# Attention block: the last three queries leave the passage as raw products and are normalised during attention's steps 3 to 10

## The chip, the cores and the metric

One Trainium2 chip, one of its NeuronCores, one launch. A core has five engines, each with its own instruction queue worked off in order: TensorE (PE: matrix products and transposes, written to PSUM), VectorE (DVE) and ScalarE (ACT) for element-wise work, GpSimd (POOL), and SyncE (SP), which here only issues DMA transfers. Engines wait for each other with semaphores. The metric is device time in microseconds (us) of the whole launch, lower is better.

## What is computed

Four layers, each added to its input x of 64 batches x 64 tokens x 512 features, all in float32. The change concerns the third, windowed attention over a paged key/value cache. Cut to what matters:

```python
x = x + x @ W[id] + b[id]                         # layer 0: a matrix per batch
x = x + x @ W1.T + low-rank update of an adapter  # layer 1
# layer 2: 8 query heads in 4 groups, head size 64
q = (x @ Wq.T), k = (x @ Wk.T), v = (x @ Wv.T)
q = q * rsqrt(mean(q * q, -1) + 1e-6) * (1 + q_norm_scale)   # per head
q = concat([q1 * cos - q2 * sin, q2 * cos + q1 * sin])       # halves rotated by position
k = the same with k_norm_scale
put k and v at their places in the cache
scores = q @ k_all.T * 256 ** -0.5, masked to a window of 256 positions
x = x + (softmax(scores) @ v_all) @ Wo.T
x = x + per-batch 64x64 matrix over the token axis + bias    # layer 3
```

## The kernel before

The 4096 tokens are 32 tiles of 128 tokens (two batches each), `NT = 32`. The program has three parts.

*The first part* (`layer0`, `layer1`, `keep_kv` and others, about 518 us) loads a matrix per batch, computes layers 0 and 1, keys and values of each tile, and the queries of tiles 0 to 24. Keys and values go to `kvd` in DRAM, turned queries to `qTd` in DRAM.

*The passage* is the loop `for i in range(NT - LATE + 1, NT - 1)` (LATE is 8): the queries of tiles 25 to 30. For each: `product` makes four matmuls of 128x512 into a PSUM bank (line 140); `turned` (lines 116 to 135) normalises and rotates: ScalarE squares it (L120), VectorE sums each head's squares (L122), ScalarE takes the root (L123), VectorE inverts it (L126) and multiplies (L128); then two half-width products with the sine (L133), one with the cosine (L134), and a sum into `qr` (L135). `turned` is a generator that stops twice, so that the caller can place its parts between other work. `turn_q` transposes `qr` with four TensorE operations (L174), copies the result with ScalarE (L177) and stores it in `qTd` (L181, SP's queue).

*Attention* has 32 steps, one per tile. Step `s` on TensorE, in this order: `scores(s)` (8 matmuls, L842), `attend(s - 1)` (48 short ones, L889), in even steps from 4 on `last(s - 4)` (layer 3), `project(s - 2)` (L917), `keys(s + 1)` (transposes of the next tile's keys, L823, L829), and `turn(s)` (transposes of the softmax weights, L875, L879). Beside it VectorE subtracts the maximum (L850), normalises the weights (`normalise`, L862, L866), adds the residual into `x3` (L921) and copies half of the transposed weights (`pT`, L876); ScalarE takes exponentials (L854) and copies keys (`kT`) and the other weights. GpSimd issues the gathers of keys and values for tile `s + 2` (`load_kv`, five indirect DMAs, L769) and adds a unit matrix to layer 3's matrix `w3` (L815). SP issues the loads of masks (`load_mask`), queries (`load_q`), residual and `w3` (`load_pair`).

Tile 31's query is made in step 0 into the one bank of the pool `pyp`, which `project` uses as well (tile `py`), its norm is spread over steps 1 to 3 and its turn is in step 5. Tile 29's turn is in step 0, tile 30's in step 4. All other PSUM tiles take turns in a ring of seven banks (`bank`). The order on all engines is the order of the program text (`manual_schedule`).

Of the kernel before, what the change touches and what calls it, by code (L numbers as in the profile page):

```python
# [12 lines left out]
F32 = mybir.dt.float32  # L13
I32 = mybir.dt.int32
AF = mybir.ActivationFunctionType
ALU = mybir.AluOpType
AX = mybir.AxisListType
# [3 lines left out]
B, T, D = 64, 64, 512  # L21
# [4 lines left out]
H, G, HD = 8, 4, 64  # L26
BLOCK, NBLK, WINDOW = 16, 257, 256
HALF = HD // 2
# [21 lines left out]
LATE = 8  # L50
NT = NTOK // 128
# [3 lines left out]
def bc(ap, shape):  # L55
    return ap.to_broadcast(list(shape))
# [3 lines left out]
def body(ctx: ExitStack, tc: tile.TileContext, a: dict, out: bass.AP):  # L60
    nc = tc.nc
    V, S, P, TE = nc.vector, nc.scalar, nc.gpsimd, nc.tensor
# [27 lines left out]
    late = ctx.enter_context(tc.tile_pool(name="late", bufs=1))  # L90
    wq = late.tile([128, KC, D], F32, name="wq")
    gain = late.tile([128, 2, 2, HALF], F32, name="gain")
    gsw = late.tile([128, 2, 2, HALF], F32, name="gsw")
    epst = late.tile([128, 1], F32, name="epst")

    ring = ctx.enter_context(tc.tile_pool(name="ring", bufs=7, space=PSUM))
    pyp = ctx.enter_context(tc.tile_pool(name="pyp", bufs=1, space=PSUM))
# [5 lines left out]
    x2s, qrs, trig = {}, {}, {}  # L103

    def gains(kind, i, pool, X):

        cg = pool.tile([128, HD], F32, name=f"cg{kind}", bufs=2 if kind else LATE)
        sg = pool.tile([128, HD], F32, name=f"sg{kind}", bufs=2 if kind else LATE)
        for t, gn, tr in ((cg, gain, "cos"), (sg, gsw, "sin")):
            X.tensor_tensor(  # L110
                t.rearrange("p (h f) -> p h f", h=2), gn[:, kind],
                bc(trig[tr, i // 8][:, i % 8 : i % 8 + 1, :], [128, 2, HALF]), ALU.mult,
            )
        return cg, sg

    def turned(ps, n, to, pool, X, kind, cg, sg):

        psv = ps[:, : n * HD].rearrange("p (h d) -> p h d", d=HD)
        sq = pool.tile([128, n, HD], F32, name=f"sq{kind}", bufs=2)
        S.activation(sq, psv, AF.Square)  # L120
        ss = pool.tile([128, n], F32, name=f"ss{kind}", bufs=2)
        V.tensor_reduce(ss, sq, AX.X, ALU.add)  # L122
        S.activation(ss, ss, AF.Sqrt, bias=epst, scale=1.0 / HD)  # L123
        yield
        rs = pool.tile([128, n], F32, name=f"rs{kind}")
        V.reciprocal(rs, ss)  # L126
        qn = pool.tile([128, n, HD], F32, name=f"qn{kind}", bufs=2)
        V.tensor_tensor(qn, psv, bc(rs[:, :, None], [128, n, HD]), ALU.mult)  # L128
        yield
        t2 = sq  # L130
        for f in range(2):
            fs, of = slice(f * HALF, (f + 1) * HALF), slice((1 - f) * HALF, (2 - f) * HALF)
            V.tensor_tensor(t2[:, :, fs], qn[:, :, of], bc(sg[:, None, fs], [128, n, HALF]), ALU.mult)  # L133
        V.tensor_tensor(qn, qn, bc(cg[:, None, :], [128, n, HD]), ALU.mult)  # L134
        X.tensor_tensor(to, qn, t2, ALU.add)  # L135

    def product(i, w, name, pool=None):
        ps = pool.tile([128, 512], F32, name="py") if pool else bank(name)
        for c in range(KC):
            TE.matmul(ps, x2s[i][:, c, :], w[:, c, :], start=c == 0, stop=c == KC - 1)  # L140
        return ps

    def parts_q(i, pq, X, cs=None):
        qr = late.tile([128, H, HD], F32, name="qr", bufs=2)
        qrs[i] = qr.rearrange("p h d -> p (h d)")
        return turned(pq, H, qr, late, X, 0, *(cs or gains(0, i, late, X)))

    def copies(to, pool, ahead):

# [16 lines left out]
    def run(parts):  # L166
        for _ in parts:
            pass

    def turn_q(i, pool=late):  # L170
        qrf = qrs.pop(i)
        pqt = bank("pqt")
        for c in range(KC):
            TE.transpose(pqt[:, c * 128 : (c + 1) * 128], qrf[:, c * 128 : (c + 1) * 128], ident)  # L174
        qT = pool.tile([128, 2, 2, 2, T], F32, name="qTs", bufs=2 if pool is late else 4)
        for gp in range(2):
            S.copy(  # L177
                qT[:, gp].rearrange("p b h t -> p h b t"),
                pqt[:, gp * 256 : (gp + 1) * 256].rearrange("p (h b t) -> p h b t", h=2, b=2),
            )  # L180
        nc.sync.dma_start(  # L181
            qTd[i * 128 : (i + 1) * 128, :], qT.rearrange("p g b h t -> p (g b h t)")
        )

    with ExitStack() as pa:
# [494 lines left out]
        for c in range(KC):  # L680
            cs = slice(c * 128, (c + 1) * 128)
# [27 lines left out]
        for g in range(NG - 1):  # L709
# [5 lines left out]
            n, m = len(tiles[g]), len(tiles[g + 1])  # L715
            for k in range(m):
                i0, i = tiles[g + 1][k], tiles[g][k * n // m] if (k + 1) % (m // n) == 0 else None
# [9 lines left out]
                if q is not None:  # L727
                    pq = product(q, wq, "pq")
# [11 lines left out]
        i = NT - LATE  # L740
        run(parts_q(i, product(i, wq, "pq"), P))
        made.append(i)
        cs = {i: gains(0, i, late, P) for i in range(NT - LATE + 1, NT)}
        while len(made) > 1:
            turn_q(made.pop(0))
# [15 lines left out]
    bp = ctx.enter_context(tc.tile_pool(name="bp", bufs=2))  # L761

    kvs, kTs, mbs, prs, pTs, oTs, qTs, pairs, x3s = {}, {}, {}, {}, {}, {}, {}, {}, {}

    def load_kv(i):
        kv = kvs[i] = kvp.tile([128, 5, 2 * G * HD], F32, name="kv")
        for n in range(5):
            at = idxn[:, n % 2, 2 * i + n // 2 :][:, :1] if n < 4 else idxh[:, i : i + 1]
            P.indirect_dma_start(  # L769
                out=kv[:, n, :], out_offset=None, in_=kvd,  # L770
                in_offset=bass.IndirectOffsetOnAxis(ap=at, axis=0),
            )
# [6 lines left out]
    def load_q(i, queue=nc.sync):  # L779
        qT = qTs[i] = bp.tile([128, 2, 2, 2, T], F32, name="qT", bufs=4)  # L780
        queue.dma_start(
            qT.rearrange("p g b h t -> p (g b h t)"), qTd[i * 128 : (i + 1) * 128, :]
        )

    def load_mask(i):
        mb = mbs[i] = bp.tile([128, 2, NPOS], F32, name="mb", bufs=3)
        for h in range(2):
            r = nc.sync.value_load(cut[0:1, 2 * i + h : 2 * i + h + 1], min_val=0, max_val=WINDOW - 1)
            if h == 0:
                nc.sync.dma_start(mb[:, 0, :], maskd[:, bass.ds(r, NPOS)])  # L790
            else:
                nc.sync.dma_start(mb[:, 1, T:], maskd[:, bass.ds(r, WINDOW)])
                nc.sync.dma_start(mb[:, 1, :T], maskd[:, WINDOW:][:, bass.ds(r, T)])
# [23 lines left out]
    def keys(i):  # L817
        kv = kvs[i]
        kT = kTs[i] = bp.tile([128, 2, 2 * NPOS], F32, name="kT")
        for gp in range(2):  # L820
            pk = bank("pkt")
            for n, c in enumerate((0, 1, 4)):
                TE.transpose(pk[:, n * 128 : (n + 1) * 128], kv[:, c, gp * 128 : (gp + 1) * 128], ident)  # L823
            S.copy(kT[:, gp, :384], pk[:, :384])
        pk = bank("pkt")
        for gp in range(2):
            for c in range(2):
                n = 2 * gp + c
                TE.transpose(pk[:, n * 128 : (n + 1) * 128], kv[:, 2 + c, gp * 128 : (gp + 1) * 128], ident)  # L829
        S.copy(kT[:, :, 384:], pk.rearrange("p (g n) -> p g n", g=2))  # L830
# [128 lines left out]
    load_q(0)  # L959
    load_mask(0)  # L960

    parts = {}
    for i in range(NT - LATE + 1, NT - 1):
        pq = product(i, wq, "pq")
        parts[i] = parts_q(i, pq, V, cs[i])
        next(parts[i])
        if i > NT - LATE + 2:
            turn_q(i - 2, bp)
        if i - 1 in parts:
            run(parts.pop(i - 1))  # L970
        next(parts[i])
    keys(0)
    load_q(1)
    load_mask(1)
    wo = bp.tile([128, KC, D], F32, name="wo", bufs=1)
    for s in range(NT):
        if s + 2 < NT:
            if s < 2:
                after_keys(s)
            load_kv(s + 2)  # L980
            load_mask(s + 2)
        if s and s + 2 < NT:
            load_q(s + 2)
        scores(s)
        if s >= 2:
            add_one(s - 2)
        if s:
            load_pair(s - 1)
            attend(s - 1)
        else:  # L990

            parts[NT - 1] = parts_q(NT - 1, product(NT - 1, wq, "pq", pyp), V, cs[NT - 1])
            turn_q(NT - 3, bp)
        if s == 2:
            next(parts[NT - 1])
        normalise(s, 0)
        normalise(s, 1)
        if s % 2 == 0 and s >= 4:
            last(s - 4)
        if s >= 2:  # L1000
            project(s - 2)
        if s + 1 < NT:
            keys(s + 1)
        if s in (4, 5):
            turn_q(NT - 6 + s, bp)
        elif s in (2, 3):

            run(parts.pop(NT - 4 + s))
        turn(s)
        if s == 0:  # L1010
            load_q(2)
            nc.sync.dma_start(wo, a["woT"].rearrange("(c p) f -> p c f", p=128))
        elif s == 1:
            next(parts[NT - 1])
    i = NT - 1
    load_pair(i)
    add_one(i - 1)
# [60 lines left out]
```

## Time and profile before

| | us |
|---|---|
| median of 3 runs | 974.5 (lowest 973.77, highest 974.64) |
| the profiled execution, with what lies around it | 969.85 |
| its span, first to last instruction | 967.9 |
| its mean granted TensorE clock | 0.995 |
| first scores of step 0, 1, 2, 3, 4 (start) | 543.78, 554.31, 565.86, 585.69, 597.45 |
| later steps, odd / even | about 11.8 / 13.6 each |

A line of the profile's timeline holds start, length, engine, line of the program, operation, `out<-in` by the program's names, shapes, how many merged instructions, and in brackets the engine's idle time before it with what ended that idle time. A matmul in float32 is recorded as two instructions. TensorE's weight loads (PEld) lie beside its matmuls.

### The profile page before, as it was taken

The numbers are of one execution on the slowest core, as the hardware profiler recorded it, in microseconds if no ns is written. First come the engines' busy times: TensorE is split into PE (matmuls) and PEld (weight loads), VectorE is DVE, ScalarE is ACT, GpSimd is POOL, SyncE is SP. The second block draws the span as 40 slices with busy tenths as digits, with TensorE's granted clock in tenths as the row PEclk, the third lists the DMA queues.
The fourth block names the chain that finished last, engine by engine and source line by source line (L and its number), as shares of the span: only waits on it lengthen the run. The fifth ranks groups of instructions, "written<-read, shape, count | busy, mean of one in ns | idle before, by whom it ended". The sixth has DMA issues, their size and how long they took to land.

```text
span 967.9 us, 17784 instructions
## 1 busy us (share of the span) xinstructions
PE 930.5 (96%) x5397; PEld 506.6 (52%) x5397; DVE 608.7 (63%) x1736; ACT 412.9 (43%) x1084; POOL 404.8 (42%) x599
## 2 busy tenths in 40 slices
PE   5999999999999999999999979999999999999998
PEld 2443443444444444444444556766666666666665
DVE  3756898878573362552226858666667776667673
ACT  0212133232341322422223666656666666666663
POOL 3344265555453454444425543344444333334400
PEclk9999999999999999999999989999999999999999
DMA  7998999999999999999953774766665566566621
GB/s 251 342 324 304 376 375 324 377 393 320 396 330 383 392 339 389 387 351 389 372 218 125 235 261 135 217 214 205 204 194 185 181 194 197 191 204 202 197 69 45
DMA packets 133344, 260.97 MB, mean 270 GB/s; under 512 B 32737, under 2 KB 41570, under 8 KB 133250
## 3 DMA queue, kind: packets, MB, share of 16 engines
q1 hardware_dynamic: 108562, 178.61, 51.6%
q0 software_dynamic: 23280, 79.84, 24.8%
q10 hardware_dynamic: 1408, 1.39, 0.5%
q8 instruction: 43, 0.70, 0.3%
q14 instruction: 51, 0.42, 0.1%
HBM read 190.29 MB, written 69.50 MB: 268 GB/s over the span
## 4 chain that ended last, share of the span: by engine, by line
PE 73%; DVE 2%; ACT 1%; issue 1%; POOL 0%; ACTq 0%
PE py L917 12%; PE po L889 8%; PE ps L842 8%; PE p L635 7%; PE pk L140 7%; PE pq L140 7%; PE p L249 6%; PE ppt L875 6%; PE pkt L823 2%; PE ppt L879 2%; PE pkt L829 1%; PE pz L929 1%; PE pqt L174 1%; DVE pT L876 1%; PE pt L273 1%; PE px L654 1%
## 5 line engine op out<-in xcount | busy, mean ns | idle before, releaser
L769 POOL DMA_INDIRECT kv<-kvd,idxn x128 | 126.6, 989 | 211.1 <-PE po L889 166.9
L854 ACT ACTIVATE pr<-pr,mx 128x320 f32<-128x320 f32 x256 | 140.1, 550 | 7.0 <-DVE mx L850 2.9
L249 PE MATMUL p<-w,xt 128*64 128x512 f32 x512 | 122.2, 606 | 8.5 <-DMA w<-in_W 8.3
L917 PE MATMUL py<-wo,oT 128*128 128x512 f32 (+1 forms) x264 | 118.3, 592 | 1.7 <-DVE qn L128 1.7
L140 PE MATMUL pk<-wkv,x 128*128 128x512 f32 x256 | 115.4, 595 | 2.1 <-ACT x L656 2.1
L155 POOL DMA_INDIRECT st<-in_kvc,cidx x68 | 69.8, 1027 | 107.4 <-DMA kvd<-st 94.3
L635 PE MATMUL p<-w,x 128*128 128x512 f32 x256 | 113.6, 601 | 0.0
L140 PE MATMUL pq<-wq,x 128*128 128x512 f32 x248 | 111.3, 593 | 0.0
L850 DVE CUSTOM_DVE_ANT_0 pr<-ps,mb 128x320 f32<-128x320 f32 x256 | 107.8, 486 | 5.5 <-PE ps L842 2.9
L842 PE MATMUL ps<-kT,qT 64*128 64x320 f32 x512 | 86.9, 459 | 10.9 <-DVE pT L876 6.3
L876 DVE COPY pT<-ppt 128x512 f32<-128x512 f32 x64 | 41.9, 687 | 73.7 <-PE ppt L879 34.5
L866 DVE TENSOR_SCALAR pr<-pr,sm 128x320 f32<-128x320 f32 x256 | 85.4, 395 | 2.2
L889 PE MATMUL po<-pT,kv 128*64 128x128 f32 (+1 forms) x1536 | 84.1, 280 | 1.5 <-issue 1.5
L274 DVE TENSOR_TENSOR x<-pt,x 128x512 f32<-128x512 f32 x32 | 22.0, 688 | 100.6 <-PE pt L273 88.4
L889 PEld LDWEIGHTS po<-pT,kv 128*64 128x64 f32 (+1 forms) x1536 | 70.5, 137 | 22.1 <-DVE mx L850 13.6
L917 PEld LDWEIGHTS py<-wo,oT 128*128 128x128 f32 x264 | 47.5, 189 | 61.5 <-issue 58.4
L635 PEld LDWEIGHTS p<-w,x 128*128 128x128 f32 x256 | 48.3, 192 | 59.0 <-issue 56.7
L249 PEld LDWEIGHTS p<-w,xt 128*64 128x64 f32 x512 | 35.9, 138 | 78.3 <-issue 72.3
L135 POOL TENSOR_TENSOR qr<-qn,sq 128x512 f32<-128x512 f32 x25 | 31.7, 1267 | 105.5 <-DVE qn L134 105.5
L140 PEld LDWEIGHTS pk<-wkv,x 128*128 128x128 f32 x256 | 46.3, 190 | 50.4 <-issue 47.3
L140 PEld LDWEIGHTS pq<-wq,x 128*128 128x128 f32 x248 | 44.9, 190 | 46.2 <-issue 46.2
L842 PEld LDWEIGHTS ps<-kT,qT 64*128 64x128 f32 x512 | 45.2, 187 | 41.4 <-DVE pT L876 20.8
(191 smaller groups left out, 1317.9 us busy)
## 6 DMA issues: line engine op xcount, KB each, us to landing
w<-in_W SPq DMA_DIRECT2D x62, 1024.0 KB
kvd<-st SPq DMA_DIRECT2D x68, 512.0 KB
xt<-in_xT SPq DMA_DIRECT2D x32, 256.0 KB
x2d<-x2n SPq DMA_DIRECT2D x32, 256.0 KB
kvd<-kvn SPq DMA_DIRECT2D x32, 256.0 KB
qTd<-qTs SPq DMA_DIRECT2D x32, 256.0 KB
qT<-qTd SPq DMA_DIRECT2D x32, 256.0 KB
x2r<-x2d SPq DMA_DIRECT2D x32, 256.0 KB
```

The costliest lines, as they stand in the source:

```text
L140: TE.matmul(ps, x2s[i][:, c, :], w[:, c, :], start=c == 0, stop=c == KC - 1)
L155: P.indirect_dma_start(out=st, out_offset=None, in_=a["kvc"].rearrange("(n r) d -> n (r d)", r=2), in_offset=bass.IndirectOffsetOnAxis(ap= ...
L249: TE.matmul(p0[hs, :], xs[i][:, c, hs], w0s[i][h][:, c, :], start=c == 0, stop=c == KC - 1)
L635: TE.matmul(p1[i], x1s[i][:, c, :], w1[:, c, :], start=c == 0, stop=False)
L769: P.indirect_dma_start(out=kv[:, n, :], out_offset=None, in_=kvd, in_offset=bass.IndirectOffsetOnAxis(ap=at, axis=0),)
L842: TE.matmul(ps[g2][:, :NPOS], qT[rows, gp, b2].rearrange("p h t -> p (h t)"), kT[rows, gp, b2 * NPOS : (b2 + 1) * NPOS], start=True, stop= ...
L850: V.tensor_tensor_reduce(out=p, in0=ps[g2][:, :NPOS], in1=mb[:, b2, :], scale=-1.0, scalar=3.0e38, op0=ALU.add, op1=ALU.min, accum_out=mx[ ...
L854: S.activation(p, p, AF.Exp, bias=mx[:, g, b2 : b2 + 1], scale=-1.0, accum_out=sm[:, g, b2 : b2 + 1],)
L866: V.tensor_scalar(p, p, sm[:, g, b2 : b2 + 1], None, ALU.mult)
L875: TE.transpose(pt[:, n * 128 : (n + 1) * 128], pr[:, g, at : at + 128], ident)
L889: TE.matmul(po[b2][g2 * 64 : (g2 + 1) * 64, gp * 128 : (gp + 1) * 128], kv[rows, n, (G + g) * HD : (G + g + 1) * HD], pT[rows, c, m * 128 ...
L917: TE.matmul(py[:, fs], oT[:, c].rearrange("p b t -> p (b t)"), wo[:, c, fs], start=c == 0, stop=c == KC - 1,)
```

## The change

Passage: tiles 25 to 28 stay, with tile 28's half products, cosine product and sum on GpSimd (new argument `M` of `turned`) instead of VectorE. After them come `keys(0)`, then tile 29's product, which ScalarE only copies to SBUF (`raw`). Tiles 30 and 31 have their products in steps 0 and 1 in `pyp`'s bank and are copied as well. Tile 28's turn is in step 0.

The norms of the three raw tiles: GpSimd squares them in steps 2 to 4, VectorE sums in steps 3 to 5, in step 6 ScalarE takes one root for all three (and one exponential of a single column) and VectorE inverts it; GpSimd multiplies and rotates in place in steps 7 to 9 (`rotate_raw`); `turn_q` is in steps 8 to 10. The buffers of the transposed queries in this part are three instead of four.

```diff
-    def turned(ps, n, to, pool, X, kind, cg, sg):
+    def turned(ps, n, to, pool, X, kind, cg, sg, M=V):
...
-            V.tensor_tensor(t2[:, :, fs], qn[:, :, of], bc(sg[:, None, fs], [128, n, HALF]), ALU.mult)
-        V.tensor_tensor(qn, qn, bc(cg[:, None, :], [128, n, HD]), ALU.mult)
+            M.tensor_tensor(t2[:, :, fs], qn[:, :, of], bc(sg[:, None, fs], [128, n, HALF]), ALU.mult)
+        M.tensor_tensor(qn, qn, bc(cg[:, None, :], [128, n, HD]), ALU.mult)
...
-        qT = pool.tile([128, 2, 2, 2, T], F32, name="qTs", bufs=2 if pool is late else 4)
+        qT = pool.tile([128, 2, 2, 2, T], F32, name="qTs", bufs=2 if pool is late else 3)
...
+    LAST = NT - 3
+    raw = bp.tile([128, 3, H, HD], F32, name="raw", bufs=1)
+    sqr = bp.tile([128, 2, H, HD], F32, name="sqr", bufs=1)
+    ssr = bp.tile([128, 3, H], F32, name="ssr", bufs=1)
+    ssr1 = bp.tile([128, 1], F32, name="ssr1", bufs=1)
+
+    def keep_raw(i, pq):
+        S.copy(raw[:, i - LAST].rearrange("p h d -> p (h d)"), pq)
+
+    def rotate_raw(i):
+        x, t2, (cg, sg) = raw[:, i - LAST], sqr[:, (i - LAST) % 2], cs[i]
+        P.tensor_tensor(x, x, bc(ssr[:, i - LAST, :, None], [128, H, HD]), ALU.mult)
+        for f in range(2):
+            fs, of = slice(f * HALF, (f + 1) * HALF), slice((1 - f) * HALF, (2 - f) * HALF)
+            P.tensor_tensor(t2[:, :, fs], x[:, :, of], bc(sg[:, None, fs], [128, H, HALF]), ALU.mult)
+        P.tensor_tensor(x, x, bc(cg[:, None, :], [128, H, HD]), ALU.mult)
+        P.tensor_tensor(x, x, t2, ALU.add)
+        qrs[i] = x.rearrange("p h d -> p (h d)")
+
     parts = {}
-    for i in range(NT - LATE + 1, NT - 1):
-        pq = product(i, wq, "pq")
-        parts[i] = parts_q(i, pq, V, cs[i])
+    for i in range(NT - LATE + 1, LAST):
+        X = P if i == LAST - 1 else V
+        parts[i] = parts_q(i, product(i, wq, "pq"), X, cs[i], X)
         next(parts[i])
         if i > NT - LATE + 2:
             turn_q(i - 2, bp)
         if i - 1 in parts:
             run(parts.pop(i - 1))
         next(parts[i])
+    run(parts.pop(LAST - 1))
     keys(0)
+    keep_raw(LAST, product(LAST, wq, "pq"))
+    turn_q(LAST - 2, bp)
...
             load_kv(s + 2)
+            if 2 <= s <= 4:
+
+                x = raw[:, s - 2]
+                P.tensor_tensor(sqr[:, s % 2], x, x, ALU.mult)
+            elif 7 <= s <= 9:
+                rotate_raw(LAST + s - 7)
...
-        else:
-
-            parts[NT - 1] = parts_q(NT - 1, product(NT - 1, wq, "pq", pyp), V, cs[NT - 1])
-            turn_q(NT - 3, bp)
-        if s == 2:
-            next(parts[NT - 1])
+        if s < 2:
+
+            keep_raw(LAST + 1 + s, product(LAST + 1 + s, wq, "pq", pyp))
+            if s == 0:
+                turn_q(LAST - 1, bp)
+        elif s == 6:
+            S.activation(ssr, ssr, AF.Sqrt, bias=epst, scale=1.0 / HD)
+
+            S.activation(ssr1, ssr[:, 0, :1], AF.Exp, scale=-1.0)
+            V.reciprocal(ssr, ssr)
...
-        if s in (4, 5):
-            turn_q(NT - 6 + s, bp)
-        elif s in (2, 3):
-
-            run(parts.pop(NT - 4 + s))
+        if 8 <= s <= 10:
+            turn_q(LAST + s - 8, bp)
+        elif 3 <= s <= 5:
+
+            V.tensor_reduce(ssr[:, s - 3], sqr[:, (s - 3) % 2], AX.X, ALU.add)
...
-        elif s == 1:
-            next(parts[NT - 1])
```

More of the change, by code (lines that the diff above doesn't have):

```diff
@@ L141, in product, with parts_q @@
         return ps
-    def parts_q(i, pq, X, cs=None):
+    def parts_q(i, pq, X, cs=None, M=V):
         qr = late.tile([128, H, HD], F32, name="qr", bufs=2)
         qrs[i] = qr.rearrange("p h d -> p (h d)")
-        return turned(pq, H, qr, late, X, 0, *(cs or gains(0, i, late, X)))
+        return turned(pq, H, qr, late, X, 0, *(cs or gains(0, i, late, X)), M)
     def copies(to, pool, ahead):
```

## The prediction

> **What bounds the kernel now.** I read the page's busy table first, then the same figures by stage, then TensorE's timeline from the passage into attention, then ScalarE's and VectorE's rows at the waits.
>
> ```profile
> PE 930.5 (96%) x5397; PEld 506.6 (52%) x5397; DVE 608.7 (63%) x1736; ACT 412.9 (43%) x1084; POOL 404.8 (42%) x599
> ...
> PE 73%; DVE 2%; ACT 1%; issue 1%; POOL 0%; ACTq 0%
> ```
>
> TensorE is the bound: the change can win only time in which TensorE waits. The stages, cut at the first scores of steps 0 and 3 (columns: length, then busy time and instructions of each engine, granted clock, DMA share, GB/s):
>
> ```profile
> 500.00:543.78 43.78, 41.85 (x135) 20.68 (x133) 28.80 (x66) 16.24 (x44) 20.25 (x36) 1.00 0.44 146
> 543.78:585.69 41.91, 36.16 (x254) 24.46 (x254) 29.24 (x99) 27.70 (x74) 20.48 (x24) 0.92 0.78 256
> 585.69:967.90 382.21, 371.06 (x3161) 250.95 (x3160) 262.35 (x910) 234.80 (x674) 137.14 (x160) 1.00 0.56 177
> ```
>
> Steps 0 to 2 lose 5.75 us to idleness and some to a clock of 0.92; the other 29 steps together lose 11. TensorE there (start, length, in brackets the idle time before and what ended it):
>
> ```profile
> 541.36 0.82 PE L823 MATMUL pkt<-ident,kv 128*128 128x128 f32 x6
> ...
> 543.78 3.26 PE L842 MATMUL ps<-kT,qT 64*128 64x320 f32 x16 [1.16 <-issue]
> 546.97 3.70 PE L140 MATMUL py<-wq,x 128*128 128x512 f32 x8
> ...
> 554.31 2.42 PE L842 MATMUL ps<-kT,qT 64*128 64x320 f32 x16
> ...
> 560.22 1.08 PE L889 MATMUL po<-pT,kv 128*64 128x128 f32 x20 [1.11 <-issue]
> ...
> 569.62 3.55 PE L842 MATMUL ps<-kT,qT 64*128 64x320 f32 x8 [2.12 <-ACT pT L876]
> 573.10 4.01 PE L889 MATMUL po<-pT,kv 128*64 128x128 f32 x48
> 578.79 3.70 PE L917 MATMUL py<-wo,oT 128*128 128x512 f32 x8 [1.68 <-DVE qn L128]
> ```
>
> A free step is step 3, from 585.69 to 597.45, by starts of its groups: scores 2.36, attend 2.49, project 3.54, keys 1.09, turn 2.28, sum 11.76. Step 2 takes 19.83. The last bracket is query 31's norm, which must empty the one `py` bank. Its ScalarE half stands ahead of step 2's exponentials, in ScalarE's timeline:
>
> ```profile
> 569.94 0.62 ACT L120 ACTIVATE sq<-py 128x512 f32<-128x512 f32 x1
> 570.58 1.28 ACT L123 ACT_TABLE_LOAD   x1
> 571.87 0.30 ACT L123 ACTIVATE ss<-ss,epst 128x8 f32<-128x8 f32 x1
> 572.19 1.28 ACT L854 ACT_TABLE_LOAD   x1
> ```
>
> The second half of the loss is another thing: from 556 to 569 the DMA engines are full and matmuls are reported late, and then the clock halves.
>
> ```profile
> 564.00:568.00 4.00, 3.31 (x21) 1.85 (x20) 1.59 (x5) 0.58 (x1) 3.11 (x4) 1.00 0.97 324
> 568.00:572.00 4.00, 2.38 (x7) 1.47 (x8) 2.10 (x5) 2.98 (x5) 0.19 (x1) 0.66 0.75 264
> 572.00:576.00 4.00, 4.00 (x31) 3.14 (x32) 2.56 (x14) 3.97 (x11) 0.00 (x0) 0.50 0.10 19
> ```
>
> **The loss in step 0 to 2, by part.** *Start:* ScalarE copies the turned keys until 544.55, VectorE ends query 30's norm at 545.53. TensorE waits 1.16 and its scores take 3.26 against 2.42: 2.0 us. *Step 1:* 554.31 to 565.86 is 11.55 for 8.22 of matmuls (11.76 without project's 3.54). Of the 3.33 lost, attend (556.66 to 561.23, 4.57 against 2.49) has 2.08, late reports; keys and turn have 1.26, waiting for a normalise that a step so short of matmuls can't cover. *Step 2:* scores run from 565.86 to 573.10, 4.9 over their 2.36; attend at half clock 1.5 over; 1.68 for `py`. Sum 8.1. Of the scores' 4.9, VectorE's wait for query 31's square (0.97) and its reduction (0.69) are 1.66. In all 13.4 to be had.
>
> **The change, part by part.**
>
> *Query 29 is only copied, behind keys(0).* Passage products 25 to 28 would end at 533.1 as now, one turn follows (0.44), keys(0) come at 533.6 instead of 541.36. The ten gathers of kv(0) and kv(1) start at 524.69 on GpSimd in both; kv(0)'s last is issued at 530.20 and landed some 3.3 us later by its semaphore, 533.5: no wait, at most some tenths. Then product 29 (3.44) and turn 27 (0.44) cover the three kT copies (0.87 and 0.62). VectorE ends its part of query 28 at 537.8, as its row for that query's `qn` has it (537.09 and 0.69). Scores(0) at 538.5 find everything: the 2.0 us come back. The exponential table (1.28) now loads behind turn 27's copies, up to 540.4, 1.1 after the first maximum; normalise(0) ends about 546.6, turn(0) starts 546.4: 0 to 1.1, I take 0.1.
>
> *Query 28 turns on GpSimd.* Two halves by the 128x256 row (0.72), two full ones by L135's 128x512 row (1.27): 3.98, behind the gathers (538.15), done 542.1. Its turn on TensorE stands behind product 30, at 544.8: hidden with 2.7 to spare. Behind it in GpSimd's queue are `seen` and kv(2)'s gathers, 542.4 instead of 544.47; keys(2) want them at 557.
>
> *Products 30 and 31 in steps 0 and 1.* Equal work, moved: product 31 from step 0 to 1, 30 from the passage to step 0. Step 1 now has 11.76 of matmuls, which covers the 1.26. The raw copies (three, by `sq` from `py` 0.62 each) replace that square, and empty `py` at once: the 1.68 is gone, and the 1.66 with the square and reduction.
>
> *Norms in steps 2 to 10.* GpSimd: three squares (1.27), three times five operations (three full, two half: 5.25), into idle stretches of 5.96 to 7.25 per step ahead of the next gathers. A square, and a product with a value repeated along 64 columns, are not in GpSimd's rows: bounds 0.33 (L815's 128x64) and 1.27 each, I take 1.27, the row of the same shape; 4 us over a step's stretch it would need to hold up gathers that are wanted two steps later. VectorE: three reductions (0.69) behind `x3` in steps 3 to 5, ahead of the pT copies, where it idles 2.3 to 3.2; off steps 2 and 3 go 2.13 each (0.75, 0.69, 0.69). ScalarE: one root and one dummy exponential with two table loads, 2 x 1.28 + 2 x 0.30 = 3.2 behind step 6's exponentials. It idles 4.14 there before the kT copies: hidden. The new wait is VectorE's reciprocal behind the root: normalise(6), `x3` and the pT copies are queued behind it. Today's step 6: exponentials end 629.8; plus 1.58 for table and root, 0.2 for the reciprocal: normalise starts 631.6 instead of 629.53 and ends 634.6. Turn(6) starts 634.25 and wants the last group at 635.6. Covered by 1 us; without cover 2.1. I take 0.5 for all of this; bounds 0 and 3.2.
>
> The Trainium skill, "ScalarE: Activation LUTs" (What ACT_TABLE_LOAD costs), adds a drain of 1.38 us to each switch and so speaks against two of them in mid-attention. The rows deny it: load at 570.58, next activation at 571.87. With it ScalarE's 3.2 would be 5.9, 1.8 beyond its idle 4.14, and the sum would be 1.8 less.
>
> *Turns of 29 to 31 in steps 8 to 10* instead of 0, 4 and 5 (query 28's takes step 0): each 0.44 TensorE, two ScalarE copies (0.65) and one 256 KB store in SP's queue, moved past the loads of the steps between. SP waits for the copies there, as in steps 4 and 5 now; mask and query loads behind are two steps ahead. No time; first use of query 29 is its load in step 27. Were the two-step lead gone, a late store would cost its 4.8 us wait.
>
> *What stays open* is the late reports (2.08 in attend, and 3.3 of the scores in step 2) and the half clock (1.5): 6.8 us. The traffic stays: wo, three gathers, masks and queries saturate DMA as now, beginning some 2 us earlier. Between all of it and none, I take that attend's 2.08 stays, that product 31 gives the copies time, and half of the other 4.8, 2.4, comes back: nearest row is step 8's start, where full DMA costs 0.62, not 2.12.
>
> **Sum** against this execution (span 967.9, 969.85 with what lies around): 2.0 + 1.26 + 1.68 + 1.66 = 6.6 sure, plus 2.4, less 0.6 = 8.4. 969.85 becomes 961.4. The runs' median is 974.5, 4.65 above the profiled one; the difference carries over: 966.1.
>
> **Rivals.** *All comes back* (12%): the stall needs query 31's norm. For: it ends when that norm is past. Against: it begins at 556.6, before it. 13.4 - 0.6: 961.7. *Less comes back* (15%): late reports and half clock cost as now and step 6 its 2.1: 6.6 - 2.6 = 4.0, 970.5. *No change* (6%): the DMA stream sets step 3's start; 5.7 MB moved from 540 to 562 wait for GpSimd, which starts only 2 us earlier; kv(3) is then late for keys(3), 974. Against: it lands 564.6, keys(3) run at 582. *Slower* (12%): GpSimd and VectorE exclude each other. 4.0 + 3.8 + 15.8 = 23.6 us of new GpSimd arithmetic. If each us costs VectorE one, steps 7 to 9 go 5.25 - 3.1 = 2.1 over its idle time each, the passage's 4.0 delays scores(0), and step 6 loses 2.1: 12.4 against 8.4, 978.5. It decides from two thirds of that. For: `w3`'s addition took 0.59 instead of 0.33 at 583.47, amid VectorE work. Against: L135's 128x512 took 1.26 beside VectorE and 1.26 alone.
>
> The "GPSIMD Engine Reference" of the Trainium skill (Specifications) has the SBUF interfaces shared, contended by VectorE operations with two SBUF inputs; by that page the slower case would be the rule. The rows beside VectorE show it once in many.
>
> **Chances.** Forecast 55%, and the rivals as above. About 0.2% (1.95 us) is what a measurement of this kernel can tell: faster 0.82, same 0.06, slower 0.12. Range: low at the full gain, 961; high past the lesser gain, 973, which leaves out the slower case and part of no change.
>
> **What would show it.** Right: scores(0) some 5 us earlier; no table load between turn(1) and exp(2); step 2 under 16 us; no wait on `qn` L128; step 6 within 0.5 of step 4; GpSimd's squares at 1.27. Wrong: VectorE's rows longer in steps 7 to 9, TensorE waiting for GpSimd at turn 28, or the clock at 0.5 for 6.8 us again.

## The result and the profile after

| | us |
|---|---|
| kernel before, median of 6 runs | 975.01 (973.77 to 976.21) |
| changed kernel, median of 6 runs | 980.78 (978.63 to 982.98) |
| ratio | 1.0056, 95% interval 1.0036 to 1.0076 |
| the changed kernel's profiled execution, its span | 980.36, 978.6 |

The change made the kernel slower, by 5.8 us; the forecast was 966.1. Two later comparisons, each on a chip of its own (e10, e18), say the same: 1.0042 (1.0023 to 1.0062) and 1.0083 (1.0054 to 1.0112). The two profiled executions differ by more than the medians, 10.7 us of span: that of the kernel before lies 5 us under its median, that of the changed one at its median. So the profiles tell where time went, and sums are made with care.

The busy table of the changed kernel's page:

```profile
PE 935.8 (96%) x5397; PEld 508.7 (52%) x5397; DVE 602.5 (62%) x1715; ACT 412.0 (42%) x1083; POOL 426.6 (44%) x621
```

TensorE is the bound as before; POOL has 22 us more, DVE 6 less. By stage (length, busy time and instructions of PE, PEld, DVE, ACT, POOL, granted clock, DMA share, GB/s), cut at the first scores of steps 0, 3, 6, 7 and 12:

```profile
540.49:585.23 44.74, 38.49 (x264) 25.65 (x263) 23.66 (x87) 24.36 (x71) 24.71 (x29) 0.89 0.74 234
585.23:623.40 38.17, 36.93 (x315) 24.89 (x315) 28.31 (x96) 23.40 (x68) 17.62 (x21) 1.00 0.60 186
623.40:642.87 19.47, 15.25 (x112) 9.02 (x111) 14.36 (x34) 12.68 (x30) 10.18 (x11) 0.89 0.56 178
642.87:709.16 66.29, 64.99 (x539) 45.60 (x539) 43.66 (x154) 39.65 (x118) 36.05 (x40) 0.98 0.59 179
709.16:975.24 266.08, 260.17 (x2203) 173.85 (x2202) 180.70 (x627) 162.96 (x464) 90.03 (x106) 1.00 0.54 172
```

| stretch, by TensorE's first scores | before | after | difference |
|---|---|---|---|
| start of step 0 | 543.78 | 540.49 | -3.3 |
| steps 0 to 2 (step 1 and step 2 alone) | 41.9 (11.55, 19.83) | 44.7 (22.10, 12.75) | +2.8 |
| steps 3 to 5 | 37.8 | 38.2 | +0.4 |
| step 6 | 13.6 | 19.5 | +5.8 |
| steps 7 to 11 | 62.9 | 66.3 | +3.4 |
| step 12 to the end | 264.3 | 266.1 | +1.8 |

The last line holds the same work in both kernels (264.3 again in e13), and so does all that lies ahead of the gathers of tile 0, which start 1.74 us later in this execution (526.43 against 524.69): these are differences between executions. The change has three places: step 0 begins some 5 us earlier counted from those gathers; steps 1 and 2 give that back; step 6 loses 5.8. Of the 3.4 in steps 7 to 11, 1.3 are the three turns moved there and 0.8 a halved clock in step 7; step 10 has 0.9 more that no experiment explains (14.88 here, 14.29 and 14.13 in e10 and e18).

Step 1 on TensorE in the changed kernel (start, length, in brackets the idle time before and what ended it):

```profile
549.86 0.60 PE L879 MATMUL ppt<-ident,pr 128*128 128x128 f32 x4
550.39 0.80 PE L842 MATMUL ps<-kT,qT 64*128 64x320 f32 x2
552.81 1.01 PE L842 MATMUL ps<-kT,qT 64*128 64x320 f32 x2 [1.62 <-issue]
556.46 1.43 PE L842 MATMUL ps<-kT,qT 64*128 64x320 f32 x2 [2.64 <-DVE pT L876]
559.22 3.56 PE L842 MATMUL ps<-kT,qT 64*128 64x320 f32 x10 [1.32 <-ACT pT L876]
562.71 2.94 PE L889 MATMUL po<-pT,kv 128*64 128x128 f32 x48
565.58 3.70 PE L140 MATMUL py<-wq,x 128*128 128x512 f32 x8
```

The scores of step 1 take 12.3 us, against 2.36 when nothing is in the way. They wait for PSUM banks that VectorE and ScalarE empty. VectorE in that time:

```profile
548.22 1.30 DVE L866 TENSOR_SCALAR pr<-pr,sm 128x320 f32<-128x320 f32 x4
555.72 0.69 DVE L876 COPY pT<-ppt 128x512 f32<-128x512 f32 x1 [6.19 <-remote]
558.64 0.69 DVE L876 COPY pT<-ppt 128x512 f32<-128x512 f32 x1 [2.23 <-PE ps L842]
```

VectorE is idle for 6.19 us although the transposes that it waits for were through by 550.5: TensorE's report, the rise of the semaphore on which VectorE and ScalarE wait, came late. The trace has that semaphore rise at 547.79, then at 552.15, 555.69 and 558.55, and within 0.03 us of the last three a waiting engine starts. (The ends of matmuls are modelled in the trace, so it can't tell a late report from transposes that really ended late.) It is the stall that the prediction left open, in another step and larger.

Step 6. The division of the weights in the kernel before:

```profile
629.74 1.40 DVE L866 TENSOR_SCALAR pr<-pr,sm 128x320 f32<-128x320 f32 x4
631.26 1.27 DVE L866 TENSOR_SCALAR pr<-pr,sm 128x320 f32<-128x320 f32 x4
```

The same step in the changed kernel's timeline, first ScalarE behind its last exponential:

```profile
630.62 1.28 ACT L1025 ACT_TABLE_LOAD   x1
631.91 0.32 ACT L1025 ACTIVATE ssr<-ssr,epst 128x24 f32<-128x24 f32 x1
632.24 1.28 ACT L1027 ACT_TABLE_LOAD   x1
633.54 0.20 ACT L1027 ACTIVATE ssr<-ssr 128x1 f32<-128x1 f32 x1
```

VectorE, which comes from the output copies of attend:

```profile
633.77 0.30 DVE L1028 RECIPROCAL ssr<-ssr 128x24 f32<-128x24 f32 x1 [3.44 <-ACT ssr L1027]
633.99 0.12 DVE L862 RECIPROCAL sm<-sm 128x4 f32<-128x4 f32 x1
634.15 2.95 DVE L866 TENSOR_SCALAR pr<-pr,sm 128x320 f32<-128x320 f32 x4
637.02 0.17 DVE L862 RECIPROCAL sm<-sm 128x4 f32<-128x4 f32 x1
637.22 4.12 DVE L866 TENSOR_SCALAR pr<-pr,sm 128x320 f32<-128x320 f32 x4
```

And GpSimd at the same time:

```profile
635.85 1.06 POOL L974 TENSOR_TENSOR raw<-raw,ssr 128x512 f32<-128x512 f32 x1
636.98 1.49 POOL L977 TENSOR_TENSOR sqr<-raw,sg 128x256 f32<-128x256 f32 x2
638.55 1.26 POOL L978 TENSOR_TENSOR raw<-raw,cg 128x512 f32<-128x512 f32 x1
639.89 1.26 POOL L979 TENSOR_TENSOR raw<-raw,sqr 128x512 f32<-128x512 f32 x1
```

Two things are to be seen. The reciprocal waits not for the root (over at 632.23) but for L1027, the dummy exponential behind the second table load: that reads `ssr`, which the reciprocal overwrites. And the division of the weights (L866, eight instructions) starts 4.4 us later than the 629.74 of the kernel before and takes 7.07 us where it took 2.67: its rows grow long where GpSimd rotates query 29, five microseconds of GpSimd in a row. VectorE gets through between its instructions only: each of the five long instructions of the division (0.67 to 1.86 us) ends 0.17 to 0.19 us behind the end of one of GpSimd's, such as 637.10 behind 636.91. GpSimd's own rows are no longer than elsewhere (1.26 to 1.28).

### The profile page after: what moved, and what is told of

It reads as the page before. It is cut to its first block, busy times and chain, and to the rows that moved or that the text cites. A ratio compares the mean times of both kernels' runs of the same rounds, so it can differ in the third digit from the quotient of the medians.

```text
span 978.6 us, 17772 instructions
## 1 busy us (share of the span) xinstructions
PE 935.8 (96%) x5397; PEld 508.7 (52%) x5397; DVE 602.5 (62%) x1715; ACT 412.0 (42%) x1083; POOL 426.6 (44%) x621
## 3 DMA queue, kind: packets, MB, share of 16 engines
q0 software_dynamic: 23280, 79.84, 24.6%
## 4 chain that ended last, share of the span: by engine, by line
PE 66%; DVE 3%; ACT 2%; DMA 2%; issue 2%; another core or an unknown queue 1%; SPq 1%; POOL 0%; ACTq 0%; DVEq 0%; POOLq 0%
PE py L917 11%; PE po L889 8%; PE ps L842 8%; PE p L635 7%; PE pk L140 6%; PE ppt L875 5%; PE pq L140 5%; PE p L249 4%; PE ppt L879 2%; PE pkt L823 2%; DMA kvd<-st 1%; PE pkt L829 1%; PE pz L929 1%; DVE pT L876 1%; DVE pr L866 1%
## 5 line engine op out<-in xcount | busy, mean ns | idle before, releaser
L140 PE MATMUL pq<-wq,x 128*128 128x512 f32 x240 | 107.7, 593 | 0.0
L842 PE MATMUL ps<-kT,qT 64*128 64x320 f32 x512 | 91.6, 472 | 14.5 <-DVE pT L876 11.6
L866 DVE TENSOR_SCALAR pr<-pr,sm 128x320 f32<-128x320 f32 x256 | 89.6, 412 | 2.3
L135 POOL TENSOR_TENSOR qr<-qn,sq 128x512 f32<-128x512 f32 x26 | 33.0, 1268 | 104.8 <-DVE qn L134 104.8
L842 PEld LDWEIGHTS ps<-kT,qT 64*128 64x128 f32 x512 | 47.4, 191 | 47.5 <-DVE pT L876 30.1
L875 PE MATMUL ppt<-ident,pr 128*128 128x128 f32 x512 | 63.3, 275 | 4.4 <-DVE pr L866 3.3
```

The costliest lines, as they stand in the source:

```text
L842: TE.matmul(ps[g2][:, :NPOS], qT[rows, gp, b2].rearrange("p h t -> p (h t)"), kT[rows, gp, b2 * NPOS : (b2 + 1) * NPOS], start=True, stop= ...
L866: V.tensor_scalar(p, p, sm[:, g, b2 : b2 + 1], None, ALU.mult)
L875: TE.transpose(pt[:, n * 128 : (n + 1) * 128], pr[:, g, at : at + 128], ident)
```

## The experiments

The experiments ran in groups: e1 to e4, e5 to e8, e9 to e12, e13 to e16, e17, e18. Each group was on one chip, beside the kernel before, and each on another chip. Two figures are read first: steps 1 and 2, and step 6. Where no interval is given (e2 to e9, e15, e16) there is one run, and its steps are read, not its total.

**Step 6.** e1 moves one line:

```diff
         elif s == 6:
             S.activation(ssr, ssr, AF.Sqrt, bias=epst, scale=1.0 / HD)
             S.activation(ssr1, ssr[:, 0, :1], AF.Exp, scale=-1.0)
-            V.reciprocal(ssr, ssr)
...
             project(s - 2)
+        if s == 6:
+            V.reciprocal(ssr, ssr)
```

> The changed kernel with one line moved: VectorE's reciprocal of the three norms stands behind step 6's division (both halves) and its residual instead of ahead of them. Theory A (step 6 loses because the division waits for the root, starts 4.6 us late at 634.1 and so runs into GpSimd's rotation, which it can't run beside): the division starts within 0.5 us of the output copies, takes 2.7 to 2.9 us instead of 7.2, step 6 (first scores to first scores) falls from 19.47 to 13.6 to 14.2, step 7 from 13.01 to 12.2 to 12.5; in all 6 to 7 us less than the changed kernel, 974 to 975.5. Theory B (GpSimd's rotation costs VectorE its length wherever it lies, also beside copies out of PSUM): the rotation then falls on the copies of step 6's turn, step 6 stays above 15 us, total above 977.

Measured: 970.74 against 972.34 before, ratio 0.9981 (0.9968 to 0.9993). Step 6 takes 13.67, step 7 12.01; the division stands at 630.74 with 1.40 and 1.27. The whole is 3 us under the expected 974, but the changed kernel was not beside it on this chip; where it was (e10, e11), the difference is 6.7 us, as expected. The rotation (636.28 to 641.6) now lies beside VectorE's copies out of PSUM:

```profile
637.51 1.29 DVE L876 COPY pT<-ppt 128x512 f32<-128x512 f32 x2 [2.26 <-PE ppt L875]
638.72 0.48 DVE L850 CUSTOM_DVE_ANT_0 pr<-ps,mb 128x320 f32<-128x320 f32 x1
```

These take what they take without it (1.29, 0.48). So theory B is out: it is the division, reading and writing SBUF, that is held up beside GpSimd's arithmetic, not VectorE as such. One line is worth the step's whole loss.

e2 leaves the rotation out: `rotate_raw` keeps `qrs[i] = x.rearrange(...)` alone.

> The changed kernel without GpSimd's rotation of the last three queries in steps 7 to 9 (the raw products are turned and stored; the three last query tiles are left without norm and rotation). The root and the reciprocal ahead of step 6's division stay. Theory A: the division still starts near 634 but takes 2.9 us instead of 7.2; step 6 falls from 19.47 to 15 to 16, what is left is the wait for the root. Theory C (the wait for the root alone makes step 6's loss, the long rows only show TensorE's and the clock's state): step 6 stays at 19 or more. Steps 8 and 10 (13.97 and 14.88 against 13.56 before) fall to 13.7 or less if the rotation costs there too, by theory B; by A they stay within 0.3 of what they are.

Measured: step 6 14.71. The division starts late as before and takes 1.84 and 1.27. Theory C is out. Steps 8 and 9 stay at 14.09 and 12.19: what they have over the kernel before is about the 0.44 of a moved turn on TensorE, not the rotation. Step 10 fell from 14.88 to 13.64, which the expectation gave to theory B; but it is 13.50 in e3 and 13.49 in e4, which have the rotation, so it tells nothing.

e3 gives the dummy another operand:

```diff
-            S.activation(ssr1, ssr[:, 0, :1], AF.Exp, scale=-1.0)
+            S.activation(ssr1, epst, AF.Exp, scale=-1.0)
```

> The changed kernel, but ScalarE's dummy exponential behind the root reads the epsilon tile instead of the roots, so that VectorE's reciprocal (which overwrites the roots) need not wait for it. Theory D (the prediction's 631.6 for the division was missed because the reciprocal waits for the second table load and the dummy, not for the root): the reciprocal starts 1.4 to 1.6 us earlier (some 1.7 us behind the last exponential instead of 3.2), the division ends just ahead of or beside the first rotation, and with theory A step 6 falls from 19.47 to 14 to 16. If the reciprocal waited for the root all along, it starts where it does now and step 6 stays at 19.

Measured: step 6 14.49. VectorE's rows:

```profile
632.13 0.30 DVE L1028 RECIPROCAL ssr<-ssr 128x24 f32<-128x24 f32 x1 [1.94 <-ACT ssr L1025]
632.36 0.12 DVE L862 RECIPROCAL sm<-sm 128x4 f32<-128x4 f32 x1
632.51 1.43 DVE L866 TENSOR_SCALAR pr<-pr,sm 128x320 f32<-128x320 f32 x4
633.86 0.16 DVE L862 RECIPROCAL sm<-sm 128x4 f32<-128x4 f32 x1
634.06 2.92 DVE L866 TENSOR_SCALAR pr<-pr,sm 128x320 f32<-128x320 f32 x4
```

The wait is 1.94 instead of 3.44 and ends with the root: 1.5 us were the dummy's. The last of the division's eight instructions still meets the rotation (1.87 us). With the collision away (e2) or the wait 1.5 shorter (e3) step 6 loses about 1 us against e1; with both 5.8.

**Steps 1 and 2, first attempt.** e4 has `kvs[3] = kvs[2]` at step 1 instead of tile 3's five gathers. (The expectations of e4 and e5 count 2.6 MB for these; by the gathers' DMA queue, 79.84 MB in the changed kernel and 78.53 in e4, they are 1.3.)

> The changed kernel without the five gathers of tile 3's keys and values: tile 3 works on tile 2's (its output is wrong for that). This takes 2.6 MB out of the DMA stream between 550 and 563 us. Theory E (TensorE's reports to the other engines come late when the DMA engines are full, and this ate what the start gained): step 1 falls from 22.1 us to 12 to 15, the copies of step 0's probabilities follow their transposes within 2.5 us, the clock stays at 1.0, step 3 starts 6 to 9 us earlier. Theory F (the stall comes from the new order of the work, VectorE's and ScalarE's queues or the missing matmuls, and the full DMA is only beside it): step 1 stays above 20 us.

Measured: step 1 21.57, but that tells nothing: tile 4's gathers took the free buffer and came in their place; the DMA share between 548 and 564 was 0.92, 0.79, 0.91, 1.05 in quarters.

e5 to e8 have e1's mended step 6 and change one thing each. e5 as e4, with tile 4's gathers held behind tile 0's output copy:

> e1_recip_behind without tile 3's gathers (it works on tile 2's keys and values; its output is wrong for that), and with tile 4's gathers held behind tile 0's output copy, as the buffers hold them in the changed kernel; in e4 they had simply moved into the freed buffer, and the DMA share between 548 and 564 was as full as ever. So 2.6 MB are really out of the DMA stream from 550 to 566. Theory E (full DMA engines make TensorE's reports late): DMA share below 0.8 from 552 to 564, scores(1) take under 5 us instead of 12.2, step 1 12 to 15 us instead of 21.9, no half clock, step 3 starts 6 to 10 us earlier than in e1 against the start of scores(0). Theory F (order of the work, not traffic): step 1 above 20 us.

e6 moves the load of `wo` from the end of step 0 to that of step 1:

> e1_recip_behind with the load of the output weights (1 MB) issued at the end of step 1 instead of step 0, so out of the stall (552 to 563) and still ahead of its first use in step 2. Theory E1 (any megabyte counts: the stall lasts until the queued bytes are through): 1 MB at some 350 GB/s is 3 us, step 1 falls from 21.9 to 18 to 20, step 2 stays within 1 us. Theory E2 (the gathers' queue makes the late reports, direct loads do not): step 1 stays within 0.7 us of 21.9. The late reports begin at 548.2, ahead of this load's issue at 554, which speaks for E2.

e7 puts `load_kv(3)` behind `attend(0)`:

```diff
             attend(s - 1)
+            if s == 1:
+                seen = bp.tile([1, 1], F32, name="seen")
+                P.tensor_copy(seen, oTs[0][0:1, 0, 0, 0:1])
+                load_kv(3)
```

> e1_recip_behind with tile 3's five gathers behind tile 0's output copy (attend(0) in step 1) instead of behind tile 1's turned keys: nothing is left out, the gathers only start some 3 to 15 us later. Theory E: the stall of step 1 shrinks as in e5, to 12 to 16 us; tile 3's and tile 4's gathers are then back to back and part of the stall comes again in step 2 (13 to 17 us instead of 12.7): together steps 1 and 2 take 26 to 31 instead of 34.6, and the whole 964 to 968. Theory F: steps 1 and 2 stay within 1 us of 34.6.

e8 gives tile 28's rotation back to VectorE:

> e1_recip_behind with query tile 28's rotation and sum on VectorE instead of GpSimd. GpSimd is then free at 538 to 540 instead of 544, and tile 2's gathers start some 4 us earlier; VectorE has 2.8 us more ahead of scores(0)'s maxima. Theory E: the ten gathers of tiles 2 and 3 are spread over more time (540 to 546 and 550 to 556), the DMA engines are less full at the stall's beginning, step 1 falls by 1 to 4 us. If the stall depends on tile 3's gathers alone (with whatever lies beside them), step 1 stays within 0.7 us of 21.9. The start of step 0 moves by less than 0.5 us.

Measured on this chip: kernel before 952.44, and e5 to e8 944.98, 945.97, 944.35, 949.36 (one run each). In all four step 1 took 11.75, even where no traffic was taken out. Step 1 of e6 as one window, then VectorE at its turn:

```profile
550.74:562.49 11.75, 11.75 (x103) 8.38 (x103) 8.45 (x30) 7.97 (x24) 8.85 (x11) 1.00 0.99 360
```

```profile
548.84 0.37 DVE L866 TENSOR_SCALAR pr<-pr,sm 128x320 f32<-128x320 f32 x1
549.14 0.68 DVE L876 COPY pT<-ppt 128x512 f32<-128x512 f32 x1
549.97 0.69 DVE L876 COPY pT<-ppt 128x512 f32<-128x512 f32 x1 [0.15 <-PE ppt L875]
```

A DMA share of 0.99, and TensorE idle for nothing: the copies follow their transposes at once. On the chip of e1 the share was 0.94 over the stall. So a full DMA alone doesn't make reports late, nor do gathers back to back (e6 has those of tiles 2 and 3 so); the chip has its part in it. The steady even steps took 12.61 here and 13.5 to 13.6 there. e8 was no gain: step 0 took 10.11 instead of 9.70.

**On one chip together.** e9 is the kernel before, e10 the changed one, e11 e1's kernel, e12 e7's.

> The kernel before, for its profile on the chip of this call. e5 to e8 ran on another chip than e1 to e4: there no report came late although the DMA share was as full (1.0 from 552 to 560), steps 1 and 2 took 11.75 each, and the kernel before took 952 us. Theory G (whether TensorE's reports come late is a matter of the chip, not of the DMA share alone): on a chip without late reports steps 0 to 2 of the kernel before take 34 to 37 us instead of 41.9, with no half clock; on a chip with them 41 to 43, the whole 970 to 976. If the kernel before loses its 4.9 us in the scores of step 2 on a chip without late reports too, query 31's norm made that loss, not the reports.

> The changed kernel beside the kernel before and e1_recip_behind on one chip. Theory A and G: step 6 takes 19 us or more with late reports, and 17 to 19.5 without (there the even steps take 12.6 and the division is 4 to 5 us late all the same and then meets the rotation). On a chip without late reports: steps 0 to 2 33.2, the whole within 2.5 us of the kernel before on either side, since 5 to 6 us are won at the start and 5 to 6 lost in step 6. With late reports: step 1 near 22, the whole 4 to 8 us over the kernel before.

> The changed kernel with the reciprocal behind step 6's division, beside the two others on one chip. Theory A: 5 to 8 us less than the changed kernel on either chip. Without late reports: 5 to 8 us less than the kernel before (all of the start's gain is kept); with them 1 to 3 us less, as in e1.

> e1_recip_behind with tile 3's gathers behind tile 0's output copy, again, since e7 ran where nothing was late. Theory E (gathers in the full DMA stream make the reports late on a chip that has late reports): step 1 falls from 21.9 to 12 to 16, steps 1 and 2 together from 34.6 to 26 to 31, the whole 3 to 8 us less than e11. Theory F: within 1 us of e11. On a chip without late reports: within 1.5 us of e11 on either side.

The chip was one with late reports. Measured against 977.19 before: e10 981.57, 1.0042; e11 974.85, 0.9978 (0.9960 to 0.9996); e12 974.46, 0.9983 (0.9964 to 1.0002).

| | step 1 | step 2 | start of step 3 |
|---|---|---|---|
| e9, before | 12.08 | 17.53 | 585.63 |
| e10, changed | 22.55 | 13.01 | 586.70 |
| e11, step 6 mended | 21.58 | 13.07 | 586.34 |
| e12, and tile 3's gathers later | 13.44 | 22.81 | 587.39 |

e9 has late reports (1.7 us of waits in attend of step 1) and 40.1 us in steps 0 to 2, so it leaves its own question open: no trace of the kernel before was taken on a chip without late reports. e12 moved the stall by one step and left its size: neither E nor F as written. GpSimd's rows of e12 fit that:

```profile
558.61 0.97 POOL L769 DMA_INDIRECT kv<-kvd,idxn  x1 [0.16 <-issue]
...
563.64 0.95 POOL L769 DMA_INDIRECT kv<-kvd,idxh  x1 [0.30 <-issue]
564.89 0.94 POOL L769 DMA_INDIRECT kv<-kvd,idxn  x1 [0.30 <-issue]
...
569.89 0.94 POOL L769 DMA_INDIRECT kv<-kvd,idxh  x1 [0.30 <-issue]
```

Tiles 3 and 4 are gathered back to back, ten gathers in 12.2 us, and step 2 stalls. In the changed kernel these are tiles 2 and 3 (544.30 to 556.6), and step 1 stalls. Back to back is not enough by itself: tiles 0 and 1 are gathered so in the passage, at a DMA share of 0.73 to 0.75, and TensorE waits 0.19 at most there. A fourth buffer is what lets a tile's gathers start at once. The last gather of tile 2 and the first of tile 3, in the kernel before and then in the changed one:

```profile
549.54 0.95 POOL L769 DMA_INDIRECT kv<-kvd,idxh  x1 [0.31 <-issue]
553.18 0.98 POOL L769 DMA_INDIRECT kv<-kvd,idxn  x1 [0.16 <-issue]
...
549.39 0.95 POOL L769 DMA_INDIRECT kv<-kvd,idxh  x1 [0.30 <-issue]
550.67 0.97 POOL L769 DMA_INDIRECT kv<-kvd,idxn  x1 [0.16 <-issue]
```

**Spacing the gathers.** e13 is e11 with one buffer less, e14 the kernel before with the same:

```diff
-    kvp = ctx.enter_context(tc.tile_pool(name="kvp", bufs=4))
+    kvp = ctx.enter_context(tc.tile_pool(name="kvp", bufs=3))
```

> e1_recip_behind with three buffers for the gathered keys and values instead of four: tile 3's five gathers then wait for tile 0's last reader (attend in step 1), tile 4's for tile 1's (attend in step 2), and so on, one tile's gathers in each step, never two back to back. Nothing is left out. Theory E (back-to-back gathers make the reports late on such a chip): no stall over 3 us in steps 1 and 2, together 24 to 28 us instead of 34.6, no half clock there, step 3 starts at 575 to 580 instead of 586, the whole 5 to 10 us less than e11, 0.985 to 0.992 of the kernel before. Theory F (the order of the work): steps 1 and 2 stay above 33. Theory G (a chip without late reports): steps 1 and 2 take 23.5 with three buffers as with four, the whole 0.990 to 0.993 of the kernel before. What could spoil it: the gathers now end some 5 us into the next step, two steps' slack becomes one.

> The kernel before with three such buffers instead of four and nothing else changed. Theory E: the late reports of steps 1 and 2 (2.1 in attend, 3.3 in the scores, 1.5 by the half clock) shrink to 2 us or less, steps 0 to 2 take 36 to 38 us instead of 41.9, the whole 0.994 to 0.997 of the kernel before; the waits for query 31's norm (1.66 and 1.68) stay. Theory F: within 0.1% of the kernel before.

> As e5 (tile 3's gathers left out, it works on tile 2's keys and values and its output is wrong for that; tile 4's held behind tile 0's output copy), on the chip of this call. Theory E: on a chip with late reports step 1 takes 12 to 14 instead of 21.9 and step 2 12 to 14. Theory F: step 1 or 2 above 20. On a chip without late reports 11.75 each, as in e5, which tells nothing.

> As e6 (the 1 MB load of the output weights at the end of step 1), on the chip of this call. Theory E1 (any megabyte counts): step 1 18 to 20 us on a chip with late reports. Theory E2 (the gathers alone count): 21.2 to 22.6. On a chip without late reports 11.75, as in e6, which tells nothing.

Measured against 971.8 before, on a chip with late reports: **e13 962.91, 0.9904 (0.9884 to 0.9925)**; e14 971.34, 1.0003 (0.9987 to 1.0018). Steps 1 and 2 of e13, and its TensorE at the place of the stall:

```profile
549.34:562.54 13.20, 12.08 (x103) 8.24 (x102) 8.17 (x30) 7.97 (x23) 5.29 (x7) 1.00 0.98 331
562.54:575.41 12.87, 12.11 (x104) 8.26 (x103) 8.83 (x31) 7.38 (x22) 5.27 (x6) 1.00 0.65 197
```

```profile
549.34 0.81 PE L842 MATMUL ps<-kT,qT 64*128 64x320 f32 x4
551.27 1.94 PE L842 MATMUL ps<-kT,qT 64*128 64x320 f32 x12 [1.12 <-DVE pT L876]
```

The clock stays at 1.00, one wait of 1.12 is left, with a DMA share of 0.98. Tile 3's gathers start at 556.04, 6.4 us behind the last of tile 2's. Step 3 starts at 575.41, ten microseconds sooner than in e1 or the changed kernel. On the same chip e16, with four buffers, took 33.7 us for steps 1 and 2, e13 26.1. In e14 step 1 took 9.48 instead of 11.55: attend's 2.08 of late reports; step 2 took 20.18 all the same, behind one late report of 3 us and then query 31's norm (`qn` 1.69, both table loads, half clock). E had 36 to 38 us for its steps 0 to 2 and 3 to 6 us of gain; it took 40.2 and gained nothing, so spacing thins the late reports out and doesn't end them. Spacing alone gains nothing, the change with step 6 mended 1.6 to 2.3 us (e1, e11), both together 8.9. e15: step 1 13.45 as E has it; step 2 18.44, over E's 14; there tile 5's gathers start 1.5 us behind tile 4's, which may be why. e16: step 1 20.97, between E1's 20 and E2's 21.2 and nearer to E2: moving this megabyte saves 0.2 to 1.6 us against the runs with tiles 2 and 3 back to back on chips with late reports (21.22 to 22.55), not 3.

e17 is the changed kernel with three buffers, e18 the changed kernel as it is:

> The changed kernel with three buffers for the gathered keys and values, and nothing else: the reciprocal still stands ahead of step 6's division. GpSimd's rotation comes behind tile 9's gathers, which now start in step 7. Theory A: the division of step 6 still starts 4 to 5 us late but takes 2.7 to 2.9 us; step 6 14.4 to 15.5 instead of 19.47, as in e2 and e3, steps 1 and 2 together 25 to 28 as in e13; the whole 0.990 to 0.994 of the kernel before. Theory C (the wait for the root alone): step 6 18 or more, the whole above 0.994.

> The changed kernel once more, beside the kernel before. On a chip without late reports (the kernel before near 951): steps 1 and 2 take 11.75 each, the gain of the start and of the norm is kept, step 6 takes 16 to 19.5 instead of 12.6 because the late division still meets GpSimd's rotation; 6 to 8 won less 4 to 7 lost: 0.996 to 1.002 of the kernel before. On a chip with late reports (the kernel before at 970 or more): step 1 near 22, step 6 near 19.4, 1.003 to 1.008, as measured twice.

e17 met a chip without late reports: 945.95 against 951.06, 0.9941 (0.9919 to 0.9962). Step 6 took 13.24 (12.61 in steps 4 and 12): the division still waits 3.36 for L1027 but takes 2.8, as theory A has it, since the rotation now stands behind gathers that start in step 7, and the loss is 0.6. e18 met one with them, 1.0083, step 1 21.22 and step 6 19.23. Whether the changed kernel as it is gains on a chip without late reports was not measured.

## Why the prediction was wrong

- *Step 0's start.* 538.5 foreseen, 540.49 measured with the gathers 1.74 late: 538.75. Right, as are tile 28's rotation (4.11 for 3.98), the squares (1.05, under the 1.27 taken) and GpSimd's rotation (5.30 for 5.25 in step 6).
- *"6.6 sure."* Each wait named did go: no table load between turn(1) and exp(2), no wait on `qn`, step 2 at 12.75. None of it was sure, since another wait ended behind it. The step that failed is "What stays open": late reports and half clock were put between nothing and what they cost before (6.8), and taken at attend's 2.08 and half of 4.8. They cost some 10 us in step 1's scores alone. "The traffic stays" looked at the sum of the traffic and not at when each tile's gathers start. What e12, e13 and e15 show in its place, on chips with late reports, is the spacing: two tiles gathered back to back in a full DMA stream stall about one step. The change moved the end of keys(1) forward, so tile 3's gathers came 2.5 us sooner and without a pause behind tile 2's (550.67, the last one of tile 2 over at 550.34; before 553.18 and 550.5).
- *The rival "no change"* had this: "the DMA stream sets step 3's start". It got 6%. Its way there was another, though: kv(3) was to be late for keys(3), and keys(3) ran at 581.86 without a wait. Step 3 started at 585.23; without the stall (e13) at 575.41, where the sum put it at 576.8.
- *Step 6, "I take 0.5 for all of this; bounds 0 and 3.2".* This step failed too: it cost 5.8. "Normalise starts 631.6" was 634.0: exponentials 0.7 later, and 1.5 for the dummy, which the working took as ScalarE's own affair. The lateness alone is worth about 1 us (e2); the rest is the collision. And the rotation was priced against VectorE's idle time as it stood before, though the same step had just moved the division towards it. A bound from a wait's length is none when the wait pushes work into a collision.
- *The rival "slower"* named the mechanism and gave it steps 7 to 9. There it cost nothing (L866 1.42 and 1.27 in step 7). It decided in step 6. The row held against it, L135 at 1.26 beside VectorE, shows GpSimd's side; the loser was VectorE. The Trainium skill, "SBUF — State Buffer" (SBUF: two separate sides), has the shared ports as an exclusive lock, against VectorE operations in a mode of two ports or with two SBUF inputs: whichever of the two starts first keeps it for its whole instruction, and the other blocks. The rows of step 6 agree that VectorE blocks, 7.07 us for 2.67 of division. Who came first they don't settle: the division's fourth instruction is recorded from 635.24, ahead of GpSimd's at 635.85, and was held until 637.10 all the same.
- *Turns.* 0.44 each left steps 4 and 5 and came into 8 to 10, as foreseen. Half a clock in step 7 (3.68 for its scores instead of 2.42) was not.

With both faults mended the kernel stands at 0.9904, 8.9 us between the medians; the forecast was 8.4, without the mending. That the two are near is in part luck: spacing the gathers also takes away late reports that the forecast left in. Where no report was late, mending step 6 alone left 6.5 and 8.1 us of gain (e6 and e7, one run each against one).

## What to carry to other kernels

When a step of yours delays an instruction, list again what it will now run beside; idle time read from the old trace holds only for the old times. An operation that works in place waits for every reader of its tile, a dummy's too: give the dummy another operand. Where two limits lie on top of each other, removing one shows little or nothing: change both before judging, and measure on more than one chip.

## What the runs showed of the hardware that was not expected

Chips differ: the kernel before took 951 to 952 us on two and 972 to 977 on four. With a DMA share of 0.99 one reported at once, another, at 0.92 to 0.94, 6 us late. What differs between the chips stays open, and so does the path on which the reports are held up; each chip was met once, so a difference between chips can't be told from one between occasions. The traces differ as well: those with late reports hold 925 to 947 of some 1040 rises of TensorE's semaphore, those without 1029 to 1039. So on the chips with late reports the trace misses events too, and whether reports are late in an execution without a trace, no run here shows.

VectorE's division of SBUF data stopped for GpSimd's arithmetic (up to 1.86 us for an instruction of 0.37); its copies from PSUM didn't (0.67 to 0.69 us each, beside it and without). The clock went to half from 638.61 to 645.44, 6.83 us from step 6 into step 7, though no wait of TensorE in step 6 was over 1.28; from 633.87 to 642.87 it ran transposes alone.
